# One product for the row sums of eight rows, a longer lag caught up near the end, and five small operations for twelve aggregations of moments

## The chip, the cores and the metric

The kernel runs on one core of one Trainium2 chip, all in float32. The metric is the device time of one execution in microseconds (us).

## The reference, cut to what matters

Two layers on `x` of shape (1, 384, 384, 128). The first is a triangle product with gates and two layer norms. The second, which is where the change lies, treats each of the 384 rows (384 positions of 128 channels) like this:

```python
left = pair @ W_left + b_left            # and W_eq, b_eq added to it
right = pair @ W_right + b_right
gate = jax.nn.sigmoid(pair @ W_gate + b_gate)
right_sum = jnp.sum(right, axis=2, keepdims=True)   # over the 384 positions of the row
out = left * right_sum * gate
out = out @ W_out + b_out
return _layer_norm(out + pair, ln_scale, ln_bias)    # over the 128 channels
```

`right_sum` is one vector of 128 channels for a row. The kernel sums pair over the positions first, and multiplies the sums by W_right.

## The kernel before, in words

The kernel has three stages: projections of the first layer (to about 1260 us), the triangle product, channel by channel (to about 1980 us), and the row stage, which goes through the 384 rows u and makes the end of the first layer and all of the second. P is 128, N is 384, C is 128, NB is 3 blocks of 128 positions, and R = 4 rows form a group that is loaded, normalised and stored together. The engines run the instructions in the order in which the code gives them (the schedule is manual), so the order of the row stage is that of the tuple `stages`: at each u, each stage is called for row u minus its lag.

One pass of the loop, with its lines:

- `load` (L505): every fourth u, SyncE starts the loads of gr, zr and xr for the group eight rows ahead (L512, L513, L522).
- `gate_product`, lag 3 (L968): VectorE (DVE) makes h = (pleft + b_left) x sg (L971).
- `turn_row`, lag 2 (L955): TensorE (PE) turns the row's pair (ptr, L560). ScalarE (ACT) copies it to pairT with an accumulated sum over the positions, which goes to column i of the group's tile `total` (L561).
- `out_weights`, lag 7 (L962): ACT scales W_out by the row's `right` column into w_o (L965).
- `layer_1`, lag 8 (L982): PE multiplies h by w_o (pf, three products, six PE passes, L987), and DVE adds pair (res, L988).
- `layer_0`, lag 0, and with it the statistics of the row eight back (L530): PE's py for row u (L537). On DVE three scalar_tensor_tensors on py (L543) alternate with three bn_stats of res (L548), then pair is made (L550), then three bn_aggr turn the statistics into mean and variance in `mv` (L553).
- `norm_factors`, lag 12 (L990): for a group of 4 rows x 3 blocks, GpSimd (POOL) makes rs = (variance + eps)^-0.5 (L995, L996) and off = -mean x rs (L998, L999).
- `normalise`, lag 13 (L1003): ACT makes res x rs + off, three a row (L1005).
- `project`, lag 2 (L1010): PE's pleft and pg from pairT (L1013, L1015), and ACT's sigmoid sg of pg (L1020). Where u is the first row of a group, the group before has all its sums: `right` adds a product of W_right with its 4 columns of `total` into the spare columns of pg's bank (L1026), and ACT copies it to the tile `right` with its bias (L1022).
- `store`, lag 17 (L1028): POOL multiplies the group by ln_scale (L1037) and adds ln_bias (L1038), and SyncE sends it out (L1042).

In the first rows, `project` and `gate_product` have one row more of lag; at row 6 `project` runs twice, and from there on the lag is as above. `behind` holds what is left of the stage before (on POOL, ACT and PE: L600 to L630, L595) and is advanced in each of the first rows, and then once in four.

[...] bn_stats leaves six numbers for a block of 128 channels: count, mean and the sum of squared deviations of its even elements, and the same of its odd ones; bn_aggr joins the two halves.

After the loop comes a tail written out by hand for the last rows. The last eight rows' statistics are made there with `statistics` (L1090, L1092) and their factors on DVE and ACT with `last_factors` (L1101 to L1110).

Of the kernel before, what the change touches and what calls it, by code (L numbers as in the profile page):

```python
# [9 lines left out]
FP = mybir.dt.float32  # L10
AF = mybir.ActivationFunctionType
ALU = mybir.AluOpType
# [8 lines left out]
def kernel(ctx: ExitStack, tc: tile.TileContext, ins, out: bass.AP):  # L21
# [89 lines left out]
    with tc.tile_pool(name="wprep", bufs=6) as wp, tc.tile_pool(name="p1s", bufs=3) as ps, tc.tile_pool(  # L111
# [49 lines left out]
        def norm_factors(n, c0=0, c1=CX, beside=nc.gpsimd):  # L161
            if n >= NT:
                return
            if n >= OLD:
                return turned_factors(n, c0, c1)
            mv, rstd, off = (tiles[n][k][:, c0:c1] for k in ("mv", "rstd", "off"))
            beside.tensor_scalar(rstd, mv[:, :, 1], EPS, None, ALU.add)
            beside.tensor_scalar(off, mv[:, :, 0], -1.0, None, ALU.mult)
            nc.gpsimd.tensor_tensor(rstd, rstd, mhalf[:, 0 : c1 - c0], ALU.pow)
            nc.gpsimd.tensor_tensor(off, off, rstd, ALU.mult)  # L170
            if c0 == 0:
                tiles[n]["zT"] = pz.tile([P, CX, C], FP, tag="zT", name=f"zn_{n}")
# [326 lines left out]
    nc.gpsimd.memset(s2, 0.0)  # L499
    LAST, AHEAD, BY_THIRDS, R, HELD = 8, 6, 6, 4, 16  # L500
    group = {}

    def load(u):
        if u % R:
            return  # L505
        load_pair(u)
        load_x(u)

    def load_pair(u):
        zr = pl.tile([P, R, NB, C], FP, tag="zr", name=f"zr_{u}")  # L510
        gr = pl.tile([P, R, NB, C], FP, tag="gr", name=f"gr_{u}")
        nc.sync.dma_start(out=gr, in_=G[u : u + R].rearrange("i (p q) c -> p i q c", q=NB))  # L512
        nc.sync.dma_start(out=zr, in_=Z[u : u + R].rearrange("i (p q) c -> p i q c", q=NB))  # L513
        g = {"z": zr, "g": gr}
        g["total"] = pl.tile([P, R], FP, tag="total", name=f"total_{u}", bufs=4)
        g["right"] = pl.tile([P, R], FP, tag="right", name=f"right_{u}", bufs=4)
        group[u // R] = g

    def load_x(u):
# [5 lines left out]
    def of(u):  # L525
        return group[u // R], u % R

    pairs = {}

    def layer_0(u, v, bank):  # L530

        now, past = 0 <= u < N, 0 <= v < N
        if now:
            g, i = of(u)
            py = bank(u)
            for q in range(NB):
                nc.tensor.matmul(  # L537
                    py[:, q, :], lhsT=g["x"][:, i, q * P : (q + 1) * P], rhs=w_o0, start=True, stop=True
                )
            pairs[u] = pairs_of.tile([P, NB, C], FP, tag="pair", name=f"pair_{u}")  # L540
        for q in range(NB):
            if now:
                nc.vector.scalar_tensor_tensor(  # L543
                    py[:, q, :], py[:, q, :], rs0[:, q, u : u + 1], g["g"][:, i, q, :], ALU.mult, ALU.mult
                )
            if past:
                b, k = of(v)
                nc.vector.bn_stats(b["st"][:, k, q, :], b["res"][:, k, q, :])  # L548
        if now:
            nc.vector.tensor_tensor(pairs[u], py, g["z"][:, i], ALU.add)  # L550
        if past:
            for q in range(NB):
                nc.vector.bn_aggr(b["mv"][:, k, q, :], b["st"][:, k, q, :])  # L553

    hs = {}

    def turn(u, ptr, pairT):
# [81 lines left out]
    with tc.tile_pool(name="p2", bufs=1, side="right", reuse_waits="tile") as p2, tc.tile_pool(  # L639
# [44 lines left out]
        def bank2(name):  # L684
            return pp2.tile([P, N], FP, tag="pm", name=name)
# [235 lines left out]
        held.close()  # L921
        work_of = ctx.enter_context(tc.tile_pool(name="work", bufs=1, reuse_waits="tile"))
        pl = ctx.enter_context(tc.tile_pool(name="p3l", bufs=3, reuse_waits="tile"))
        pairs_of = ctx.enter_context(tc.tile_pool(name="p3r", bufs=12, reuse_waits="tile"))
        behind, rest = None, [NB - 2]
        for ib in range(NB):
            for d in range(C - LAST, C):
                if ib == NB - 1 and d == C - LAST:
                    load_x(0)
                    load_x(R)  # L930
                product(d, ib)
                if behind:
                    advance(behind)
                if ib == NB - 2 and d in (C - LAST, C - LAST + 1):
                    load_pair((d + LAST - C) * R)
                if ib == NB - 1 and d in (C - 4, C - 3):
                    layer_0(d + 4 - C, -1, lambda u: bank2(f"py_{u}").rearrange("p (q c) -> p q c", q=NB))
                if ib == NB - 1 and d == C - 2:
                    turn(0, bank2("ptr3_0"), pairs_of.tile([P, N], FP, tag="pair", name="pairT_0"))
            add_squares()  # L940
            behind = (deviation(ib), deviation(ib, rest), None)[ib]
# [4 lines left out]
    with tc.tile_pool(name="p3s", bufs=4, reuse_waits="tile") as ps, tc.tile_pool(  # L946
# [4 lines left out]
        name="p3q", bufs=2, space=PSUM, reuse_waits="tile"  # L951
    ) as plp, tc.tile_pool(name="p3f", bufs=2, space=PSUM, reuse_waits="tile") as pfp:
        wos = {}

        def turn_row(u):  # L955
            if u:
# [10 lines left out]

        def gate_product(u):  # L968
            pleft, sg = hs[u]
            h = ps.tile([P, N], FP, tag="h", name=f"h_{u}", bufs=8)  # L970
            nc.vector.scalar_tensor_tensor(h, pleft, b_left, sg, ALU.add, ALU.mult)  # L971
            hs[u] = h

        def results(u):
            g, i = of(u)
            if i == 0:
                g["res"] = pg3.tile([P, R, NB, C], FP, tag="res", name=f"res_{u}")
                g["st"] = pg3.tile([P, R, NB, 6], FP, tag="st3", name=f"st3_{u}")
                g["mv"] = pg3.tile([P, R, NB, 2], FP, tag="mv3", name=f"mv3_{u}")
            return g, i  # L980

        def layer_1(u):  # L982
# [5 lines left out]
            nc.vector.tensor_tensor(g["res"][:, i], pf, pairs.pop(u), ALU.add)  # L988

        def norm_factors(u):  # L990
            if u % R:
                return
            g, _ = of(u)
            rs = pg3.tile([P, R, NB], FP, tag="rs1", name=f"rs1_{u}")
            nc.gpsimd.tensor_scalar(rs, g["mv"][:, :, :, 1], EPS, None, ALU.add)  # L995
            nc.gpsimd.tensor_tensor(rs, rs, mhalf[:, 0 : R * NB].rearrange("p (r q) -> p r q", r=R), ALU.pow)  # L996
            off = pg3.tile([P, R, NB], FP, tag="off", name=f"off_{u}")
            nc.gpsimd.tensor_tensor(off, g["mv"][:, :, :, 0], rs, ALU.mult)  # L998
            nc.gpsimd.tensor_scalar(off, off, -1.0, None, ALU.mult)  # L999
            g["rs"], g["off"] = rs, off  # L1000

        def normalise(u):
            g, i = of(u)  # L1003
# [6 lines left out]
        def project(u):  # L1010
            pairT = hs[u]
            pleft = plp.tile([P, N], FP, tag="pleft", name=f"pleft_{u}")
            nc.tensor.matmul(pleft, lhsT=w_left, rhs=pairT, start=True, stop=True)  # L1013
            pg = pgp.tile([P, 512], FP, tag="pg", name=f"pg_{u}")
            nc.tensor.matmul(pg[:, 0:N], lhsT=w_gate, rhs=pairT, start=True, stop=True)  # L1015
            g = group.get(u // R - 1) if u % R == 0 else None
            if g:
                right(g, pg)
            sg = ps.tile([P, N], FP, tag="sg3", name=f"sg3_{u}")
            nc.scalar.activation(sg, pg[:, 0:N], AF.Sigmoid, bias=b_gate)  # L1020
            if g:
                nc.scalar.activation(g["right"], pg[:, N : N + R], AF.Identity, bias=b_right)  # L1022
            hs[u] = pleft, sg

        def right(g, pg):
            nc.tensor.matmul(pg[:, N : N + R], lhsT=w_right, rhs=g["total"], start=True, stop=True)  # L1026

        def store(u, n=R):  # L1028

# [11 lines left out]
        def send(u, n, res):  # L1041
            nc.sync.dma_start(out=y_out[u : u + n].rearrange("i (p q) c -> p i q c", q=NB), in_=res)  # L1042

        stages = (
            (load, -2 * R), (gate_product, 3), (turn_row, 2), (out_weights, 7), (layer_1, 8), (layer_0, 0),
            (norm_factors, 12), (normalise, 13), (project, 2), (store, 17),
        )
        load(2 * R)
        behind = chain(
            rest_of_deviation(*rest, lambda: pfp.tile([P, N], FP, tag="pf", name="pr_1")),  # L1050
            last_deviation(NB - 1, lambda: pfp.tile([P, N], FP, tag="pf", name="pr_2")),
        )
        for u in range(2, N):
            for stage, lag in stages:

                if stage in (gate_product, project):
                    if u < lag + R:
                        lag += 1
                    elif u == lag + R:
                        stage(u - lag - 1)  # L1060
                if stage is layer_0:
                    stage(u, u - 8, lambda u: pyp.tile([P, NB, C], FP, tag="py", name=f"py_{u}"))
                elif 0 <= u - lag < N:
                    stage(u - lag)
                if stage is layer_1 and (u < 12 or u % R == 1):
                    advance(behind)

# [6 lines left out]
        def bank(u):  # L1074
            pool, tag = ((pyp, "py"), (pfp, "pf"), (plp, "pleft"))[(D - 1 - u) // 2]
            banks[u] = pool.tile([P, NB, C], FP, tag=tag, name=f"end_{u}")
            return banks[u]
# [66 lines left out]
            nc.vector.tensor_tensor(res, banks[u], over(ln_b, NB), ALU.add)  # L1144
            nc.sync.dma_start(out=y_out[u].rearrange("(p q) c -> p q c", q=NB), in_=res)

        norm_factors(D - 12)
        turn_row(D - 2)
        gate_product(D - 3)
        out_weights(D - 7)  # L1150
        layer_1(D - 8)
        statistics(D - 8)
        turn_row(D - 1)
        out_weights(D - 6)
# [89 lines left out]
```

## Time and profile before

| | |
|---|---|
| runs of the kernel | median 3152.47 us of 3 (3152.08 to 3152.94) |
| the profiled execution | 3152.62 us, its span 3150.8 us |
| granted TensorE clock | 0.998 |
| busy, of the span: PE, DVE, ACT, POOL | 99%, 93%, 70%, 81% |
| the row stage, 2200 to 2400 us: busy of 200 us, PE, DVE, ACT, POOL | 200.00, 200.00, 175.58, 192.13 |
| the same stretch: weight loads on PE; DMA's share | 162.19; 0.78 |
| DRAM traffic in the row stage | 256 to 267 GB/s |

The time of an execution is its span (first to last instruction) and about 1.8 us around it. In a row of the profile, `L543 DVE SCALAR_TENSOR_TENSOR py<-py,acc,gr` is an instruction of line 543 on DVE that writes tile py from py, acc and gr; then come a count, the busy time, the mean duration in ns, and the idle time ahead of it with what ended that. PE multiplies float32 in two passes, each with its weight load (PEld), so a product has two PE instructions, and three products have six. In a timeline the first number is the start, the second the duration, both in us. Instructions overlap a little: on DVE the next one starts some 0.08 us before the end of the one ahead, so that the cost of an instruction is the time from its start to the next one's start. The chain of waits is the work that set the end, followed back from the last instruction.

### The profile page before, as it was taken

What the parts mean: (1) busy time and instruction counts of PE and PEld (TensorE: products, weight loads), DVE (VectorE), ACT (ScalarE), POOL (GpSimd) and SP (SyncE); (2) the same over time, 40 slices, a digit from 0 to 9 for tenths busy, and PEclk for the clock granted to TensorE, in tenths of its full rate; (3) what the DMA queues carried; (4) which work ended last, traced back from release to release, by engine and by line L of the source; (5) the groups of instructions that cost most, each with busy time, mean ns of one, the idle gap of its engine ahead of it and who ended that gap; (6) DMA issues with size and microseconds to landing.
All of it is one profiled execution on the core that took longest, in us unless ns stands there. A gap on an engine that the chain in (4) does not pass through costs nothing.

```text
span 3150.8 us, 57517 instructions
## 1 busy us (share of the span) xinstructions
PE 3130.0 (99%) x15723; PEld 2229.0 (71%) x15723; DVE 2928.8 (93%) x9353; ACT 2219.7 (70%) x5816; POOL 2564.9 (81%) x2753
## 2 busy tenths in 40 slices
PE   9999999999999999999999999999999999999998
PEld 6555555555555555788888887788888888888886
DVE  7999999999999998788888888999999999999999
ACT  7666666666666666555555554688888888888888
POOL 7888888888888886777777775599999998888887
PEclk9999999999999999999999999999999999999999
DMA  7999999999999999999999999677777777777774
GB/s 250 370 363 371 371 363 372 360 351 365 368 371 363 371 359 346 352 328 327 326 331 329 326 322 308 229 264 264 259 269 259 270 260 268 265 258 271 257 271 153
DMA packets 427742, 983.15 MB, mean 312 GB/s; under 512 B 40848, under 2 KB 335376, under 8 KB 382240
## 3 DMA queue, kind: packets, MB, share of 16 engines
q1 hardware_dynamic: 385344, 752.64, 68.8%
q0 software_dynamic: 41504, 226.58, 18.1%
q8 instruction: 130, 2.13, 0.3%
q14 instruction: 188, 1.54, 0.1%
q10 hardware_dynamic: 576, 0.26, 0.0%
HBM read 526.39 MB, written 452.98 MB: 311 GB/s over the span
## 4 chain that ended last, share of the span: by engine, by line
PE 98%; ACT 1%; DMA 1%; DVE 0%; POOL 0%; issue 0%; SPq 0%; DVEq 0%; POOLq 0%
PE py L537 8%; PE pgo L271 8%; PE pf L987 8%; PE pleft L1013 8%; PE pg L1015 8%; PE pga L309 8%; PE pb L309 8%; PE pgb L309 8%; PE pa L309 8%; PE pm L840 7%; PE ptr L560 4%; PE be L840 4%; PE al L840 4%; PE ga L840 4%; PE pm L702 1%; PE p L840 1%
## 5 line engine op out<-in xcount | busy, mean ns | idle before, releaser
L1005 ACT ACTIVATE res<-res,off,rs 128x128 f32<-128x128 f32 x1134 | 474.8, 485 | 1.0
L317 ACT ACTIVATE sga<-pga,c_L_conv_bga 128x512 f32<-128x512 f32 x288 | 197.9, 687 | 326.2 <-PE pga L309 326.1
L543 DVE SCALAR_TENSOR_TENSOR py<-py,acc,gr 128x128 f32<-128x128 f32 x1152 | 391.1, 340 | 0.6
L271 PEld LDWEIGHTS pgo<-wC_go,xT 128*128 128x128 f32 x2208 | 287.5, 192 | 124.8 <-issue 65.3
L1038 POOL TENSOR_TENSOR res<-res,r_L_conv_ln_bias 128x1536 f32<-128x1536 f32 (+1 forms) x96 | 326.8, 3404 | 7.5
L1020 ACT ACTIVATE sg<-pg,c_L_conv_b_gate 128x384 f32<-128x384 f32 x384 | 223.3, 581 | 150.7 <-PE pg L1015 100.7
L1037 POOL TENSOR_TENSOR res<-res,r_L_conv_ln_scale 128x1536 f32<-128x1536 f32 (+1 forms) x96 | 327.0, 3406 | 0.5 <-ACT res L1005 0.5
L235 POOL TENSOR_TENSOR acc<-xt,r_L_conv_b_out 128x2048 f32<-128x2048 f32 x72 | 326.0, 4527 | 0.2
L537 PE MATMUL py<-w_o,xr 128*128 128x128 f32 x2304 | 320.0, 275 | 0.0
L987 PE MATMUL pf<-w_o,h 128*128 128x128 f32 x2280 | 316.7, 275 | 0.0
L548 DVE BATCH_NORM_STATS2 st<-res 128x6 f32<-128x128 f32 x1128 | 313.3, 278 | 0.0
L1013 PE MATMUL pleft<-pairT,m_L_conv_W_left 128*128 128x384 f32 x768 | 311.5, 487 | 0.3 <-ACT pairT L561 0.3
L1015 PE MATMUL pg<-pairT,m_L_conv_W_gate 128*128 128x384 f32 x768 | 310.6, 486 | 0.0
L355 DVE SCALAR_TENSOR_TENSOR bt<-pb,c_L_conv_bb,sgb 128x512 f32<-128x512 f32 x288 | 216.1, 750 | 83.5 <-ACT sgb L317 38.6
L537 PEld LDWEIGHTS py<-w_o,xr 128*128 128x128 f32 x2304 | 288.3, 192 | 0.8
L271 PE MATMUL pgo<-wC_go,xT 128*128 128x128 f32 x2208 | 288.5, 275 | 0.0
L840 PE MATMUL pm<-ab 128*128 128x384 f32 x708 | 286.3, 486 | 1.5 <-ACT pm L783 1.5
L987 PEld LDWEIGHTS pf<-w_o,h 128*128 128x128 f32 x2280 | 284.6, 192 | 0.5
L309 PE MATMUL pga<-xT,wC_ga 128*128 128x512 f32 x552 | 282.6, 594 | 0.0
L309 PE MATMUL pb<-xT,wC_b 128*128 128x512 f32 x552 | 281.9, 592 | 0.0
L309 PE MATMUL pgb<-xT,wC_gb 128*128 128x512 f32 x552 | 281.9, 592 | 0.0
L309 PE MATMUL pa<-xT,wC_a 128*128 128x512 f32 x552 | 281.9, 592 | 0.0
(245 smaller groups left out, 8221.5 us busy)
## 6 DMA issues: line engine op xcount, KB each, us to landing
A<-at POOLq DMA_DIRECT2D x144, 512.0 KB, 10.4
Z<-acc POOLq DMA_DIRECT2D x72, 1024.0 KB, 10.8
gr<-G SPq DMA_DIRECT2D x96, 768.0 KB, 6.2
zr<-Z SPq DMA_DIRECT2D x96, 768.0 KB, 7.8
xr<-X SPq DMA_DIRECT2D x96, 768.0 KB, 8.4
X<-xd SPq DMA_DIRECT2D x381, 192.0 KB, 6.7
xt<-in_x_dram SPq DMA_DIRECT2D x71, 1024.0 KB, 7.9
out_dram<-res SPq DMA_DIRECT2D x93, 768.0 KB, 4.2
```

Of the source, the lines that this page charges most:

```text
L235: nc.gpsimd.tensor_tensor(zb, tiles[n]["x"], over(b_out, CX), ALU.add)
L271: nc.tensor.matmul(pgo[:, c, :], lhsT=zT[:, c, :], rhs=wT["go"], start=True, stop=True)
L309: nc.tensor.matmul(pk, lhsT=wT[k], rhs=zT, start=True, stop=True)
L537: nc.tensor.matmul(py[:, q, :], lhsT=g["x"][:, i, q * P : (q + 1) * P], rhs=w_o0, start=True, stop=True)
L543: nc.vector.scalar_tensor_tensor(py[:, q, :], py[:, q, :], rs0[:, q, u : u + 1], g["g"][:, i, q, :], ALU.mult, ALU.mult)
L840: nc.tensor.matmul(columns(to), lhsT=x, rhs=y, start=start, stop=True, skip_group_check=True)
L987: nc.tensor.matmul(pf[:, q, :], lhsT=h[:, q * P : (q + 1) * P], rhs=w_o, start=True, stop=True)
L1005: nc.scalar.activation(g["res"][:, i, q, :], g["res"][:, i, q, :], AF.Identity, bias=g["off"][:, i, q : q + 1], scale=g["rs"][:, i, q : q ...
L1013: nc.tensor.matmul(pleft, lhsT=w_left, rhs=pairT, start=True, stop=True)
L1015: nc.tensor.matmul(pg[:, 0:N], lhsT=w_gate, rhs=pairT, start=True, stop=True)
L1037: nc.gpsimd.tensor_tensor(flat, flat, over(ln_s, n * NB), ALU.mult)
L1038: nc.gpsimd.tensor_tensor(flat, flat, over(ln_b, n * NB), ALU.add)
```

## The change

Three things change in the row stage.

1. **The right product** is made once for eight rows up to row 328, and once for four after that. Two groups share one tile of 8 sums and one of 8 right columns.
2. **The lag** of `out_weights`, `layer_1` and all that follows is four rows longer (a row's layer_1 comes 12 rows after its layer_0 instead of 8), since a row's right column may come four rows later. The four rows are caught up: at u = 341, 348, 355 and 362, `layer_1` is called for two rows, with two `out_weights` one row ahead and two `normalise` six rows behind. The tables `due` and `plan` say which rows are due at which u. `normalise` stands one row further behind `layer_1` than before, and so does `store`; at u = 383, `normalise` is called twice. `h` has 12 buffers instead of 8, `pair` 14 instead of 12.
3. **The moments.** Instead of three bn_aggr for each row, a generator `moments` joins the halves for a whole group (12 columns) in five DVE operations and one Square on ACT, spread over the row that ends the group and the next one: after each of the calls of `gate_product`, `out_weights` and `layer_1`, it is advanced by a step. Two of its intermediate results lie in the spare columns of py's bank, which is now taken whole. `norm_factors` on POOL is an add, the pow and a multiplication (three operations instead of four). The last eight rows still use bn_aggr.

```diff
+    BY_FOUR, CAUGHT_UP = 328, (330, 338, 346, 354)
+    def octet(u):
+        return 2 * R if u < BY_FOUR else R
+    def products_at(v):
+        return v + 12 - sum(v >= k for k in CAUGHT_UP)
...
-        g["total"] = pl.tile([P, R], FP, tag="total", name=f"total_{u}", bufs=4)
-        g["right"] = pl.tile([P, R], FP, tag="right", name=f"right_{u}", bufs=4)
+        n = octet(u)
+        if u % n == 0:
+            g["sums"], g["rights"] = (
+                pl.tile([P, 2 * R], FP, tag=k, name=f"{k}_{u}", bufs=4)[:, 0:n] for k in ("total", "right")
+            )
+        else:
+            g["sums"], g["rights"] = (group[u // R - 1][k] for k in ("sums", "rights"))
+        g["total"], g["right"] = (g[k][:, u % n : u % n + R] for k in ("sums", "rights"))
...
-            if past:
-                b, k = of(v)
+            for b, k in map(of, past):
                 nc.vector.bn_stats(b["st"][:, k, q, :], b["res"][:, k, q, :])
         if now:
             nc.vector.tensor_tensor(pairs[u], py, g["z"][:, i], ALU.add)
-        if past:
-            for q in range(NB):
-                nc.vector.bn_aggr(b["mv"][:, k, q, :], b["st"][:, k, q, :])
+        if past and past[-1] % R == R - 1:
+            ending[0] = moments(past[-1], whole[:, N:])
+            advance(ending[0])
...
+        def moments(u, spare):
+            n = R * NB
+            other_mean, other_part = (spare[:, k * n : k * n + n].rearrange("p (r q) -> p r q", r=R) for k in (0, 1))
+            g, _ = of(u)
+            mean, part, other_m, other_p = (g["st"][:, :, :, k] for k in (1, 2, 4, 5))
+            var, off, apart = (pg3.tile([P, R, NB], FP, tag=k, name=f"{k}_{u}") for k in ("rs1", "off", "apart"))
+            g["rs"], g["off"], g["apart"] = var, off, apart
+            nc.vector.tensor_scalar(other_mean, other_m, -0.5, None, ALU.mult)
+            yield
+            nc.vector.scalar_tensor_tensor(apart, other_mean, 2.0, mean, ALU.mult, ALU.add)
+            nc.vector.scalar_tensor_tensor(off, mean, -0.5, other_mean, ALU.mult, ALU.add)
+            nc.vector.tensor_scalar(other_part, other_p, 1.0 / C, EPS, ALU.mult, ALU.add)
+            yield
+            nc.scalar.activation(apart, apart, AF.Square, scale=0.5)
+            yield
+            nc.vector.scalar_tensor_tensor(var, part, 1.0 / C, other_part, ALU.mult, ALU.add)
+            yield
...
         def norm_factors(u):
-            if u % R:
-                return
             g, _ = of(u)
-            rs = pg3.tile([P, R, NB], FP, tag="rs1", name=f"rs1_{u}")
-            nc.gpsimd.tensor_scalar(rs, g["mv"][:, :, :, 1], EPS, None, ALU.add)
+            rs, off = g["rs"], g["off"]
+            nc.gpsimd.tensor_tensor(rs, rs, g["apart"], ALU.add)
             nc.gpsimd.tensor_tensor(rs, rs, mhalf[:, 0 : R * NB].rearrange("p (r q) -> p r q", r=R), ALU.pow)
-            off = pg3.tile([P, R, NB], FP, tag="off", name=f"off_{u}")
-            nc.gpsimd.tensor_tensor(off, g["mv"][:, :, :, 0], rs, ALU.mult)
-            nc.gpsimd.tensor_scalar(off, off, -1.0, None, ALU.mult)
-            g["rs"], g["off"] = rs, off
+            nc.gpsimd.tensor_tensor(off, off, rs, ALU.mult)
...
-            g = group.get(u // R - 1) if u % R == 0 else None
+            g = group[u // R - 1] if u and u % octet(u - 1) == 0 else None
             if g:
                 right(g, pg)
...
         def right(g, pg):
-            nc.tensor.matmul(pg[:, N : N + R], lhsT=w_right, rhs=g["total"], start=True, stop=True)
+            n = g["sums"].shape[1]
+            nc.tensor.matmul(pg[:, N : N + n], lhsT=w_right, rhs=g["sums"], start=True, stop=True)
...
-            (load, -2 * R), (gate_product, 3), (turn_row, 2), (out_weights, 7), (layer_1, 8), (layer_0, 0),
-            (norm_factors, 12), (normalise, 13), (project, 2), (store, 17),
+            (load, -2 * R), (gate_product, 3), (turn_row, 2), (out_weights, None), (layer_1, None), (layer_0, 0),
+            (norm_factors, None), (normalise, None), (project, 2), (store, None),
         )
+        for v in range(N):
+            u = products_at(v)
+            plan(out_weights, u - 1, v)
+            plan(layer_1, u, v)
+            plan(normalise, u + 6 if u + 6 < N else N - 1 if u + 5 < N else u + 5, v)
+            if v % R == 0:
+                plan(norm_factors, products_at(v + R - 1) + 1, v)
+                plan(store, u + 10, v)
...
+                if stage in (gate_product, out_weights, layer_1):
+                    advance(ending[0])
...
-        norm_factors(D - 12)
         turn_row(D - 2)
         gate_product(D - 3)
+        advance(ending[0])
         out_weights(D - 7)
+        advance(ending[0])
         layer_1(D - 8)
+        advance(ending[0])
+        norm_factors(D - 12)
         statistics(D - 8)
```

More of the change, by code (lines that the diff above doesn't have):

```diff
@@ L528, with layer_0 @@
     pairs = {}
-    def layer_0(u, v, bank):
-        now, past = 0 <= u < N, 0 <= v < N
+    def layer_0(u, past, bank):
+        now = u < N
         if now:
             g, i = of(u)
-            py = bank(u)
+            whole = bank(u)
+            py = whole[:, 0:N].rearrange("p (q c) -> p q c", q=NB)
             for q in range(NB):
@@ L550, in layer_0 @@
             nc.vector.tensor_tensor(pairs[u], py, g["z"][:, i], ALU.add)
-        if past:
-            for q in range(NB):
-                nc.vector.bn_aggr(b["mv"][:, k, q, :], b["st"][:, k, q, :])
+        if past and past[-1] % R == R - 1:
+            ending[0] = moments(past[-1], whole[:, N:])
+            advance(ending[0])
+    ending = [iter(())]
     hs = {}
@@ L923 @@
         pl = ctx.enter_context(tc.tile_pool(name="p3l", bufs=3, reuse_waits="tile"))
-        pairs_of = ctx.enter_context(tc.tile_pool(name="p3r", bufs=12, reuse_waits="tile"))
+        pairs_of = ctx.enter_context(tc.tile_pool(name="p3r", bufs=14, reuse_waits="tile"))
         behind, rest = None, [NB - 2]
@@ L936 @@
                 if ib == NB - 1 and d in (C - 4, C - 3):
-                    layer_0(d + 4 - C, -1, lambda u: bank2(f"py_{u}").rearrange("p (q c) -> p q c", q=NB))
+                    layer_0(d + 4 - C, (), lambda u: bank2(f"py_{u}"))
                 if ib == NB - 1 and d == C - 2:
@@ L969, in gate_product @@
             pleft, sg = hs[u]
-            h = ps.tile([P, N], FP, tag="h", name=f"h_{u}", bufs=8)
+            h = ps.tile([P, N], FP, tag="h", name=f"h_{u}", bufs=12)
             nc.vector.scalar_tensor_tensor(h, pleft, b_left, sg, ALU.add, ALU.mult)
@@ L977, in results @@
                 g["res"] = pg3.tile([P, R, NB, C], FP, tag="res", name=f"res_{u}")
-                g["st"] = pg3.tile([P, R, NB, 6], FP, tag="st3", name=f"st3_{u}")
-                g["mv"] = pg3.tile([P, R, NB, 2], FP, tag="mv3", name=f"mv3_{u}")
+                g["st"] = pg3.tile([P, R, NB, 6], FP, tag="st3", name=f"st3_{u}", bufs=2)
+                if u >= N - 2 * R:
+                    g["mv"] = pg3.tile([P, R, NB, 2], FP, tag="mv3", name=f"mv3_{u}", bufs=2)
             return g, i
@@ L1021, in project @@
             if g:
-                nc.scalar.activation(g["right"], pg[:, N : N + R], AF.Identity, bias=b_right)
+                n = octet(u - 1)
+                nc.scalar.activation(g["rights"], pg[:, N : N + n], AF.Identity, bias=b_right)
             hs[u] = pleft, sg
         def right(g, pg):
-            nc.tensor.matmul(pg[:, N : N + R], lhsT=w_right, rhs=g["total"], start=True, stop=True)
+            n = g["sums"].shape[1]
+            nc.tensor.matmul(pg[:, N : N + n], lhsT=w_right, rhs=g["sums"], start=True, stop=True)
         def store(u, n=R):
@@ L1044, with plan @@
         stages = (
-            (load, -2 * R), (gate_product, 3), (turn_row, 2), (out_weights, 7), (layer_1, 8), (layer_0, 0),
-            (norm_factors, 12), (normalise, 13), (project, 2), (store, 17),
-        )
+            (load, -2 * R), (gate_product, 3), (turn_row, 2), (out_weights, None), (layer_1, None), (layer_0, 0),
+            (norm_factors, None), (normalise, None), (project, 2), (store, None),
+        )
+        due = {}
+        def plan(stage, u, v):
+            due.setdefault((stage, u), []).append(v)
+        for v in range(N):
[6 more added lines that the diff above has]
+                plan(store, u + 10, v)
         load(2 * R)
@@ L1053 @@
         for u in range(2, N):
+            past = due.get((layer_1, u), ())
             for stage, lag in stages:
@@ L1060 @@
                         stage(u - lag - 1)
-                if stage is layer_0:
-                    stage(u, u - 8, lambda u: pyp.tile([P, NB, C], FP, tag="py", name=f"py_{u}"))
+                if lag is None:
+                    for v in due.pop((stage, u), ()):
+                        stage(v)
+                elif stage is layer_0:
+                    stage(u, past, lambda u: pyp.tile([P, 512], FP, tag="py", name=f"py_{u}"))
                 elif 0 <= u - lag < N:
                     stage(u - lag)
+                if stage in (gate_product, out_weights, layer_1):
+                    advance(ending[0])
                 if stage is layer_1 and (u < 12 or u % R == 1):
```

## The prediction

> **What bounds the kernel now.** First the page's busy line and its chain of waits, for the engine that sets the end.
>
> ```profile
> PE 3130.0 (99%) x15723; PEld 2229.0 (71%) x15723; DVE 2928.8 (93%) x9353; ACT 2219.7 (70%) x5816; POOL 2564.9 (81%) x2753
> ...
> PE 98%; ACT 1%; DMA 1%; DVE 0%; POOL 0%; issue 0%; SPq 0%; DVEq 0%; POOLq 0%
> ```
>
> PE is the chain for 98% of the span. The change touches only the row stage (from about 1980 us), so next the chain of waits cut to its end, which lists PE's pieces one after the other (start, length):
>
> ```profile
> 3056.05 0.65 PE pleft L1013 x2
> 3056.69 0.65 PE pg L1015 x2
> 3057.34 0.33 PE ptr L560 x3
> 3057.66 0.67 PE pf L987 x6
> 3058.34 0.67 PE py L537 x6
> 3059.01 0.65 PE pleft L1013 x2
> 3059.65 0.65 PE pg L1015 x2
> 3060.30 0.12 PE pg L1026 x2
> ...
> 3062.14 0.65 PE pleft L1013 x2
> ```
>
> From one pleft to the next a row takes 2.96 us without a gap; the row that holds the right product takes 3.13. Four rows: 3 x 2.960 + 3.133 = 12.013, or 3.003 a row. One right product costs 0.173 us (in the trace's nanoseconds, 3133 less 2960), not the 0.12 of its own piece. Then DVE's timeline near the end, because DVE is the nearest second:
>
> ```profile
> 3118.26 0.30 DVE L553 BATCH_NORM_AGGREGATE mv<-st 128x2 f32<-128x6 f32 x3
> 3118.48 0.58 DVE L971 SCALAR_TENSOR_TENSOR h<-pleft,c_L_conv_b_left,sg 128x384 f32<-128x384 f32 x1
> ...
> 3121.48 0.58 DVE L971 SCALAR_TENSOR_TENSOR h<-pleft,c_L_conv_b_left,sg 128x384 f32<-128x384 f32 x1
> ...
> 3134.17 0.17 DVE L1106 SCALAR_TENSOR_TENSOR t<-r,few 128x12 f32<-128x12 f32 x1
> 3134.37 0.17 DVE L1107 TENSOR_TENSOR few<-t,few 128x12 f32<-128x12 f32 x1
> 3134.58 0.18 DVE L1108 SCALAR_TENSOR_TENSOR few<-few,r 128x12 f32<-128x12 f32 x1
> 3134.79 0.17 DVE L1109 COPY rs<-few 128x12 f32<-128x12 f32 x1
> 3134.88 0.16 DVE L1110 SCALAR_TENSOR_TENSOR off<-mv,few 128x12 f32<-128x12 f32 x1
> 3134.95 0.69 DVE L1090 BATCH_NORM_STATS2 st<-end 128x6 f32<-128x128 f32 x3
> ```
>
> From h to h DVE takes 3.00 us with no idle time (3.005 over the stage, from the nanoseconds). So DVE is full too, level with PE: taking work from PE alone would gain nothing. The three aggregations of a row cost 0.22 (3118.26 to 3118.48). The lower rows price an operation on 12 columns: 0.07 to 0.09 from start to start where it needn't wait for the one before (L1109, L1110), 0.20 to 0.21 where it must (L1106 to L1108).
>
> **Part 1, right products on PE.** Before, the loop makes one at each of rows 4, 8, ... 380: 95. After: at 8, 16, ... 328 (41), then at 332 ... 380 (13): 54. Its 8 columns instead of 4 I take as free: the 128x4 product's time is weight loads (2 x 190 ns busy) and a fixed part. 41 x 0.173 = **-7.1 us**, if nothing else becomes the bound.
>
> **Part 2, moments on DVE.** Removed for four rows: 4 x 0.22 = 0.88. Added: five operations. In the built program the first (after pair) and the fourth (after off) wait for the DVE instruction just before them; the other three have work between. Bounds: 5 x 0.073 = 0.37 to 5 x 0.21 = 1.05. I take 3 x 0.08 + 2 x 0.20 = 0.64, by those rows. DVE then needs 12.02 - 0.88 + 0.64 = 11.78 for four rows, 2.945 a row, against PE's 2.960 + 0.173/8 = 2.982. So PE stays the bound with 0.037 a row to spare, and part 1's gain is real. DVE becomes the bound when the five cost more than 0.88 - (12.02 - 11.93) = 0.79, which is 0.158 each.
>
> [...]
>
> The Square that ACT gets per group is the price of the 128x12 sd (start to start 0.06 to 0.09); ACT waits 134.9 us for pg's products in 373 rows from 2010 to 3120 us, 0.36 a row, and that hides it. The sigmoid's table has Square in it: L579 loads it at 1971.95 and the L722 squares follow at 1973.37 without a load. POOL loses L999 (0.26 and a gap of 0.08) and swaps L995 (0.25) for an add near L998's 0.21. Its four-row round up to about row 200 was 12.0 (pow 2.30, scale and shift 6.92, L628 1.67, rest) and becomes 11.6, within PE's 11.93. The factors are ready some 2 us before ACT's first normalise, which now stands a row later. SP's store moves one row back ahead of the next loads, which have eight rows of lead; the res buffers' 16 rows of lead shrink to 14 where rows are caught up, against a life of some 40 us. All these cost nothing; if that cover fails, a wait of about 1 us per group there shows on ACT.
>
> **Part 3, four rows of lag at the start.** Rows 8 to 11 lose their pf (0.67 each), paid later in four rows (341, 348, 355, 362) with two: +2.7. What comes back at the start is less, because without pf nothing covers ACT's pairT:
>
> ```profile
> 1990.66 0.28 PE L1026 MATMUL pg<-total,m_L_conv_W_right 128*128 128x4 f32 x2
> ...
> 1992.33 0.91 PE L1013 MATMUL pleft<-pairT,m_L_conv_W_left 128*128 128x384 f32 x2 [0.34 <-ACT pairT L561]
> ```
>
> This is row 7 of before, the one without a pf at the final lag: PE waits. The loop is sg to pairT 0.48, pairT to pleft 0.73 (1991.60 to 1992.33), pleft to the next sg 1.59 (to 1993.92): 2.80 against 2.96. So rows 8 to 10 save 0.16 each, row 11 (after a right product) nothing, and row 7 saves 0.37 for row 4's right product, of which 0.17 is counted. Net 2.7 - 0.5 - 0.2 = **+2.0** (bounds 0, if those rows ran at the 2.29 of rows 3 and 4, and 2.7).
>
> **Part 4, ACT in the catch-up.** Rows 347, 354, 361 and 368 get two rows of normalise: three more L1005, 1.16 from start to start (3127.09 to 3128.24 in the tail), and the first three a second w_o, 0.29 (3118.48 to 3118.77). Less ACT's idle 0.38 of a plain row (ahead of the sg at 2501.44), plus the Square's 0.09, sg comes 1.2 late. pairT has 0.26 to spare before pleft (end 2502.49, 0.16 from end to pleft as at 1992.33, pleft at 2502.91), and the second pf of 348, 355 and 362 adds 0.67: about 0.2 to 0.3 of PE wait each, more where Square waits for a DVE that the double row made late. Row 369 has no second pf: 0.9 - 0.3 = 0.6. Sum **+1.5**, bounds 0.5 and 4.5 (each lateness in full).
>
> **Part 5, the last row.** Row 383 also gets two normalises. Its sg is on the path (3123.54, idle 0.28 before it), and pairT, ptr, pleft and ACT to the end follow it: 1.16 - 0.28 = **+0.9**. The later factors of the last full group (pow 2.3) are ready before ACT's normalise at 3132.35.
>
> Sum: -7.1 + 2.0 + 1.5 + 0.9 = -2.7 on the profiled execution's 3152.62 (span 3150.8 and 1.8 around it): 3149.9. It stands 0.15 above the median of 3152.47, so the forecast is **3149.8**.
>
> **Rivals.**
> A, the edges are nearly free: early rows at 2.29 as rows 3 and 4 show, no stall in the catch-up; -7.1 + 0.9: 3146.3, down to 3145.4 without part 5. Against it: rows 3 and 4 still have the longer lag to pleft, and row 7 waits.
> B, slower: all five DVE operations pay the dependent 0.21. DVE then needs 12.02 - 0.88 + 1.05 = 12.19, 3.047 a row, 0.044 over today's pace for some 370 rows: +16, near 3168. [...] Against it: three have another operation between. It decides from 0.158 each on.
> C, ACT's lateness hits PE in full: +4.5 instead of 1.5: 3152.8, no change.
>
> **Chances.** Forecast 0.64, A 0.18, C 0.10, B 0.08. About 0.2% (6.3 us) is what a measurement of this kernel can tell from no change: faster needs under 3146.2, nearly half of A with a little of the forecast's tail, 0.10; slower is B, 0.08; the rest 0.82. The range leaves out B and the low end of A: 3145.8 to 3152.9.
>
> **What would show it.** Right: pleft to pleft 2.96 in seven rows of eight and 3.13 in the eighth; DVE with idle time ahead of h or py; the operations of the first and fourth moments at 0.2 and the others near 0.08; pleft waiting for pairT in rows 8 to 11; sg late in the four catch-up rows. Wrong: a PE wait on DVE in the steady rows, an h-to-h of 3.0 or more without idle time (B), or POOL's factors ending ACT's idle time ahead of normalise.

## The result, and the profile after

The changed kernel takes 3160.62 us (median of 10 runs, 3160.26 to 3161.26), the kernel before, run beside it, 3152.68 (10 runs). The ratio is 1.0026, with a 95% interval of 1.0016 to 1.0035: 8 us slower, where 2.7 us faster was forecast, and above the top of the range (3152.9). The profiled execution's span is 3158.6 us.

The page's busy line and chain of waits:

```profile
PE 3129.4 (99%) x15641; PEld 2222.3 (70%) x15641; DVE 2917.0 (92%) x8695; ACT 2232.6 (71%) x5869; POOL 2533.6 (80%) x2659
...
PE 95%; ACT 1%; POOL 1%; DVE 1%; DMA 1%; issue 0%; ACTq 0%; SPq 0%; DVEq 0%; POOLq 0%
```

PE's busy time is 0.6 us lower in a span 7.8 us longer, and POOL and DVE, with nothing in the chain before, now hold 1% each: 39 and 36 us in which they are on the path, 4 and 6 before. The steady rows are not where it happened. PE's timeline near 2500 us (start, duration):

```profile
2498.90 0.81 PE L1042 MATMUL pleft<-pairT,m_L_conv_W_left 128*128 128x384 f32 x2
...
2501.86 0.81 PE L1042 MATMUL pleft<-pairT,m_L_conv_W_left 128*128 128x384 f32 x2
...
2503.15 0.28 PE L1057 MATMUL pg<-total,m_L_conv_W_right 128*128 128x8 f32 x2
...
2504.99 0.81 PE L1042 MATMUL pleft<-pairT,m_L_conv_W_left 128*128 128x384 f32 x2
...
2507.95 0.81 PE L1042 MATMUL pleft<-pairT,m_L_conv_W_left 128*128 128x384 f32 x2
```

A row takes 2.96 us, one with a right product 3.13, and those now come every eighth row: as forecast, the 128x8 product costs what the 128x4 one did. To find where the time went, line up the two traces by rows: when does pleft of row r start, less when it did before? The row stage itself starts up to 1 us earlier or later from one profile to the next, so the difference at row 0 is taken off. The table counts rows by their pleft. Where the text below says "row 348" of a stretch on PE or of a call, it means the pass u = 348 of the loop, whose pleft is that of row 346. In us:

| row | 12 | 328 | 347 | 354 | 361 | 370 | 382 | end of span |
|---|---|---|---|---|---|---|---|---|
| changed kernel | -0.8 | -7.1 | -5.3 | -2.0 | +4.5 | +6.7 | +7.4 | +7.7 |
| e1, store first | -0.8 | -7.1 | -5.4 | -3.8 | -2.3 | -0.8 | -0.1 | +0.1 |
| e2, five res buffers | -0.9 | -7.4 | -5.7 | -4.1 | -1.8 | +1.4 | +2.2 | +2.4 |
| e3, moments alone | 0.0 | 0.0 | 0.0 | 0.0 | 0.0 | 0.0 | +0.7 | +0.9 |
| e4, e1 with bn_aggr | -0.8 | -2.7 | -0.6 | +0.6 | +1.9 | +2.7 | +3.7 | +3.7 |
| e5, e1 and Square later | -0.8 | -7.1 | -5.5 | -4.6 | -3.7 | -3.1 | -2.3 | -2.3 |
| e6, e1 and longer lag at the start | -2.8 | -9.8 | -8.0 | -6.4 | -4.9 | -3.5 | -2.7 | -2.5 |
| e7, e1 and normalise spread | -0.8 | -7.1 | -5.8 | -4.7 | -3.6 | -3.0 | -3.0 | -2.7 |
| e8, all four edits | -2.9 | -9.8 | -8.4 | -7.8 | -7.1 | -6.8 | -6.5 | -6.0 |

Up to row 328 the changed kernel is 7.1 us ahead. Between there and row 370, the catch-up, it loses 13.7, of which 2.7 are the four pf that were put off. Eleven us are waits. The waits of the stage from 2010 to 3120 us name most of them (engine, line, what it waited for: us in all, times, longest):

```profile
DVE res L1022 <- DMA out_dram<-res: 6.8, 2, 3.5
...
PE pf L1021 <- DVE rs L985: 4.2, 2, 2.4
...
DVE res L1022 <- PE pf L1021: 2.2, 1, 2.2
...
ACT res L1034 <- POOL off L1029: 1.7, 1, 1.7
```

DVE waits for a store: the buffer that a new group's res is to go into has not been sent out. PE then waits for DVE. None of this was in the kernel before. The wait of 2.2 us that the view puts down to PE's pf is a store's too: that row's pf had ended at 3081.00, and res starts at 3084.01, 0.12 us after the store of the buffer's last group landed, as it does in the other two (3.2 and 3.5 us). So DVE stands 9.0 us for stores, in three places. At one of these places, in the timeline of DVE and PE:

```profile
3033.93 0.56 DVE L1022 TENSOR_TENSOR res<-pf,pair 128x384 f32<-128x384 f32 x1 [3.22 <-DMA out_dram<-res]
...
3034.41 0.16 DVE L985 SCALAR_TENSOR_TENSOR rs<-st,py 128x12 f32<-128x12 f32 x1
...
3034.64 0.91 PE L1021 MATMUL pf<-w_o,h 128*128 128x128 f32 x6 [1.88 <-DVE rs L985]
```

And why was the buffer late? It is that of group 328, whose last normalise ended at 3012.93. POOL's timeline:

```profile
3006.32 3.45 POOL L1069 TENSOR_TENSOR res<-res,r_L_conv_ln_bias 128x1536 f32<-128x1536 f32 x1
3009.74 0.21 POOL L1027 TENSOR_TENSOR rs<-rs,apart 128x12 f32<-128x12 f32 x1
3010.03 2.28 POOL L1028 TENSOR_TENSOR rs<-rs,mhalf 128x12 f32<-128x12 f32 x1
3012.39 0.21 POOL L1029 TENSOR_TENSOR off<-off,rs 128x12 f32<-128x12 f32 x1
3019.51 0.21 POOL L1027 TENSOR_TENSOR rs<-rs,apart 128x12 f32<-128x12 f32 x1 [6.91 <-DVE rs L985]
3019.80 2.27 POOL L1028 TENSOR_TENSOR rs<-rs,mhalf 128x12 f32<-128x12 f32 x1
3022.14 0.21 POOL L1029 TENSOR_TENSOR off<-off,rs 128x12 f32<-128x12 f32 x1
3022.32 3.45 POOL L1068 TENSOR_TENSOR res<-res,r_L_conv_ln_scale 128x1536 f32<-128x1536 f32 x1
```

Two sets of factors follow each other, 332's and 336's. Ahead of the second POOL stands idle for 6.91 us until DVE has group 336's last row, and behind it, in POOL's order, waits group 328's scale, whose data has lain ready since 3012.93. It starts 9.4 us late. In the steady rows factors come at u = 0 and scales at u = 2 (modulo 4). In the catch-up the due rows move: `plan(norm_factors, products_at(v + R - 1) + 1, v)` puts 336's factors at u = 350, `plan(store, u + 10, v)` puts 328's store at u = 350 too, and the tuple of stages has norm_factors first. The same meets groups 336 and 344, whose scales start 12.3 and 12.5 us after their data. It doesn't meet 352: its store comes at u = 371, the factors of 360 at u = 372, and its scale is 3.5 us late only because POOL is still behind.

### The profile page after: what moved, and what is told of

Same layout as the page of the kernel before. It is cut to its first block, busy times and chain, and to the rows that moved or that the text cites. A ratio compares the mean times of both kernels' runs of the same rounds, so it can differ in the third digit from the quotient of the medians.

```text
span 3158.6 us, 56583 instructions
## 1 busy us (share of the span) xinstructions
PE 3129.4 (99%) x15641; PEld 2222.3 (70%) x15641; DVE 2917.0 (92%) x8695; ACT 2232.6 (71%) x5869; POOL 2533.6 (80%) x2659
## 4 chain that ended last, share of the span: by engine, by line
PE 95%; ACT 1%; POOL 1%; DVE 1%; DMA 1%; issue 0%; ACTq 0%; SPq 0%; DVEq 0%; POOLq 0%
PE pgo L271 8%; PE pga L309 8%; PE pa L309 8%; PE pb L309 8%; PE pgb L309 8%; PE py L552 7%; PE pleft L1042 7%; PE pf L1021 7%; PE pg L1044 7%; PE pm L855 7%; PE ptr L575 4%; PE be L855 4%; PE al L855 4%; PE ga L855 4%; PE pm L717 1%; PE p L855 1%
## 5 line engine op out<-in xcount | busy, mean ns | idle before, releaser
L558 DVE SCALAR_TENSOR_TENSOR py<-py,acc,gr 128x128 f32<-128x128 f32 x1152 | 404.9, 351 | 0.9
L562 DVE BATCH_NORM_STATS2 st<-res 128x6 f32<-128x128 f32 x1128 | 326.4, 290 | 0.0
```

The costliest lines, as they stand in the source:

```text
L558: nc.vector.scalar_tensor_tensor(py[:, q, :], py[:, q, :], rs0[:, q, u : u + 1], g["g"][:, i, q, :], ALU.mult, ALU.mult)
```

## The experiments

Three theories of the loss. P: POOL's order in the catch-up. Q: ACT's doubled work holds PE, and POOL only follows (rival C of the prediction, larger). R: four res buffers are too few in any order. Two more runs (e3, e4) test what the prediction got right, that DVE and PE had to be relieved together, and four (e5 to e8) what is left of the loss. Run beside e1 to e4, the kernel before takes 3152.06 us, beside e5 to e8 3152.09, and beside the changed kernel it took 3152.68; so a run is set against the changed kernel by its distance from the kernel before. The intervals are some 0.09% to each side, 2.8 us: gains of 2.4 to 2.8 us are no more than that, and what shows them is the place in the table where they arise.

**e1, store first.** In the changed kernel:

```diff
-            (norm_factors, None), (normalise, None), (project, 2), (store, None),
+            (store, None), (norm_factors, None), (normalise, None), (project, 2),
```

> The changed kernel with one edit: in the tuple of stages, store stands ahead of norm_factors, so that on POOL the scale of a finished group goes ahead of the factors of a later one. Theory P (POOL's order): in the changed kernel the scale of groups 328, 336, 344 and 352 starts some 9 to 14 us after its data is ready, because the factors of the group two further on stand ahead of it and wait for their last row; the four res buffers then come free late, and DVE waits for the store. Without that, the catch-up (rows 336 to 370) loses the 2.7 us of the moved pf and some 1.5 us of ACT lateness instead of 13.7: 3150 to 3152.5 us. Theory Q (ACT): the doubled w_o and normalise hold PE by themselves and POOL only follows: 3159 to 3161. Theory R (four res buffers are too few for 14 rows in any order): DVE still waits for the store, 3156 to 3160.

Measured 3152.26 us (11 runs; before 3152.06, ratio 1.0001, 0.9992 to 1.0010): 0.2 us slower than the kernel before instead of 7.9. One tuple's order is worth 7.7 us, or 7.5 by the table. POOL in the same place:

```profile
3011.38 0.21 POOL L1029 TENSOR_TENSOR off<-off,rs 128x12 f32<-128x12 f32 x1
3011.98 3.47 POOL L1068 TENSOR_TENSOR res<-res,r_L_conv_ln_scale 128x1536 f32<-128x1536 f32 x1 [0.39 <-ACT res L1034]
...
3018.93 0.23 POOL L1027 TENSOR_TENSOR rs<-rs,apart 128x12 f32<-128x12 f32 x1
```

The scale starts as soon as ACT is done, and 336's factors, placed behind it, start 0.7 us after DVE starts the last operation on their data (3018.19). DVE waits for no store any more. P stands; Q and R fall as the main cause. What is left of the catch-up's loss (6.3 from row 328 to 370, of which 2.7 for pf) is 3.6 us: the subject of e5 and e7.

**e2, five res buffers.** In the changed kernel, POOL's order as it was:

```diff
-                g["res"] = pg3.tile([P, R, NB, C], FP, tag="res", name=f"res_{u}")
+                g["res"] = pg3.tile([P, R, NB, C], FP, tag="res", name=f"res_{u}", bufs=5)
```

> The changed kernel with five res buffers instead of four, POOL's order as it is. Theory P and theory R: DVE no longer waits for the store of the group four back, so most of the 11 us of stalls goes: 3150.5 to 3153.5 us; the late scales on POOL remain and cost nothing but the length of the queue; what differs from the run with store first is the hold of the factors behind late scales (ACT waited 1.7 us for off). Theory Q: 3159 to 3161.

Measured 3154.51 (ratio 1.0008, 0.9999 to 1.0017): 2.5 us slower than the kernel before, 5.5 better than the changed kernel, 1.0 outside the expectation and 2.3 short of e1. DVE's waits for the store are gone, and the remaining way shows in the waits from 3000 to 3125 us:

```profile
ACT res L1034 <- POOL off L1029: 5.5, 3, 2.0
...
PE pleft L1042 <- ACT pairT L576: 3.8, 5, 1.1
```

POOL's late scales also hold the next factors; ACT waits for those, and its pairT comes late for PE. So the one inversion had two ways to PE, through the buffers and through the factors, and a fifth buffer closes only one.

**e3, the moments alone.** The changed kernel with `BY_FOUR = 0` and `return v + 8` in `products_at`: a right product for every four rows, no longer lag, no catch-up.

> The change of the moments alone: a right product for four rows and the lag of 8 as before, no catch-up; moments, normalise and store one row later as in the changed kernel. Theory (PE is the bound at 3.003 us a row, DVE was level with it): DVE gets idle time, PE's pace stays, 0 to 1 us from the kernel before, 0.9 more for the double normalise of the last row: 3152.0 to 3154.0 us. Rival (PE was held by DVE, 3.005 a row, or by its PSUM buffers): faster by 1 to 7 us. Rival (the moments themselves cost PE through py's bank or ACT's Square): slower by more than 2 us.

Measured 3152.88 (ratio 1.0003, 0.9994 to 1.0011). By rows it runs level with the kernel before to the last row (PE 3.003 us a row in both), and loses 0.7 to 0.9 in the tail, at row 383's double normalise. DVE's relief by itself gives nothing, since PE takes its 3.003 anyway. DVE now follows PE at a fixed distance: h starts 2.25 us after its row's pleft from row 60 to row 324, where before that distance crept up from 2.39 to 2.60 in the first 180 rows.

**e4, bn_aggr in place of the moments.** e1 with the old lines: in `layer_0`

```diff
-        if past and past[-1] % R == R - 1:
-            ending[0] = moments(past[-1], whole[:, N:])
-            advance(ending[0])
+        for b, k in map(of, past):
+            for q in range(NB):
+                nc.vector.bn_aggr(b["mv"][:, k, q, :], b["st"][:, k, q, :])
```

and `norm_factors` as before, with `mv` for every group.

> The run with store first, but with the twelve bn_aggr of before in place of the moments: right product for eight rows, lag 12 and catch-up remain. Theory (DVE is level with PE in the kernel before, so taking work from PE alone gains nothing): DVE sets the pace at 3.005 us a row, and the 7 us of right products don't show; 3152 to 3156 us. Rival (PE alone is the bound, DVE's missing idle time is only its queue): as fast as the run with store first, within 0.7 us.

Measured 3155.73 (ratio 1.0012, 1.0004 to 1.0021), 3.5 us behind e1. It shows how a lead is lost: from row 20 to row 100 PE does run at 2.982 us a row, and DVE's h falls behind pleft from 2.52 to 4.30 us. PE turns a row's pair two rows after DVE makes it. At row 20 the transposes (ptr) start 1.9 us after the pair's end, at row 60 0.9, and from row 100 on 0.15 to 0.16. In the timelines of DVE and PE at one of the later rows:

```profile
2932.68 0.60 DVE L564 TENSOR_TENSOR pair<-py,zr 128x384 f32<-128x384 f32 x1
...
2933.43 0.52 PE L575 MATMUL ptr<-ident,pair 128*128 128x128 f32 x3
```

So the distance between pair and ptr is used up. From row 220 to row 324 PE's pace is 3.002, near DVE's 3.005. The difference at row 328 is 2.7 us instead of 7.1; from there to row 370 it loses 5.5, e1 6.3. With e3 this shows that the two halves of the change need each other.

**e5, Square later.** e1, with ACT's Square moved behind the row's normalise:

```diff
-            nc.scalar.activation(apart, apart, AF.Square, scale=0.5)
-            yield
             nc.vector.scalar_tensor_tensor(var, part, 1.0 / C, other_part, ALU.mult, ALU.add)
             yield
+            nc.scalar.activation(apart, apart, AF.Square, scale=0.5)
+            yield
...
-                if stage in (gate_product, out_weights, layer_1):
+                if stage in (gate_product, layer_1, normalise):
```

(and one more yield after the first operation, and norm_factors behind normalise). It aims at this. ACT's timeline in e1, three rows after a double row:

```profile
3016.10 0.40 ACT L998 ACTIVATE w_o<-m_L_conv_W_out,right 128x128 f32<-128x128 f32 x1
3017.53 0.21 ACT L983 ACTIVATE apart<-apart 128x12 f32<-128x12 f32 x1 [1.03 <-DVE apart L979]
...
3018.80 0.56 ACT L1049 ACTIVATE sg<-pg,c_L_conv_b_gate 128x384 f32<-128x384 f32 x1
```

And PE's timeline in e1 for the same row:

```profile
3016.53 0.81 PE L1042 MATMUL pleft<-pairT,m_L_conv_W_left 128*128 128x384 f32 x2
3020.12 0.91 PE L1042 MATMUL pleft<-pairT,m_L_conv_W_left 128*128 128x384 f32 x2 [0.29 <-ACT pairT L576]
```

Three rows after a double row DVE is still late; ACT stands 1.03 us at Square, sg and pairT are late, and PE's row, which holds a right product, takes 3.59 instead of 3.13.

> The run with store first, and ACT's Square moved behind the row's normalise (the fourth DVE step then goes before it, and norm_factors behind normalise), so that ACT no longer stands at Square for a DVE that a double row made late. Theory S (Square in ACT's order is what stalls rows 351, 358 and 365, 0.3 to 0.6 us each, with some more in the double rows themselves): 1.2 to 2 us faster than the run with store first, 3150.3 to 3151.1. Rival (ACT has no time for its work in these rows in any order): within 0.5 us of it. Rival (the later factors make normalise wait): slower.

Measured 3149.86 (ratio 0.9993, 0.9984 to 1.0001), 2.4 us under e1, a little more than expected. Rows 351, 358 and 365, which took 3.59, 3.29 and 3.26 us in e1, take 3.13, 2.96 and 2.96.

**e6, longer lag at the start.** e1, and in the loop

```diff
-                    if u < lag + R:
+                    if u < lag + 2 * R:
                         lag += 1
-                    elif u == lag + R:
+                    elif u == lag + 2 * R:
```

> The run with store first, with the longer lag of project and gate_product kept for four rows more at the start (up to row 10 instead of 6). Theory (rows without a pf at the final lag are held by the loop sg, pairT, pleft at 2.80 us; with one row more of lag PE runs them at 2.29): rows 7 to 9 come back to 2.29, 1.5 us faster than the run with store first, 3150.5 to 3151. Rival (the first rows are held by something else, DVE or the loads): within 0.5 us of it.

Measured 3149.49 (ratio 0.9992, 0.9983 to 1.0001), 2.8 us under e1, where 1.5 was expected. PE's timeline in the changed kernel's first rows:

```profile
1994.91 0.91 PE L1042 MATMUL pleft<-pairT,m_L_conv_W_left 128*128 128x384 f32 x2 [0.24 <-ACT pairT L576]
...
1997.70 0.91 PE L1042 MATMUL pleft<-pairT,m_L_conv_W_left 128*128 128x384 f32 x2 [0.24 <-ACT pairT L576]
```

And PE's timeline in the same stretch of e6:

```profile
1989.37 0.81 PE L1042 MATMUL pleft<-pairT,m_L_conv_W_left 128*128 128x384 f32 x2
...
1991.66 0.81 PE L1042 MATMUL pleft<-pairT,m_L_conv_W_left 128*128 128x384 f32 x2
```

2.79 us a row with a wait against 2.29 without. The table's rows 5 to 8 gain, four of them and not three, so 2.0 by row 12. Another 0.6 is three small waits of 0.2 to 0.3 (near rows 24, 112 and 185) that the changed kernel and e1 have and e6 doesn't; their cause was not followed.

**e7, normalise spread.** e1, with at most four of normalise's activations in a row, in their order, and row 370's last two in ACT's idle times of the tail:

```diff
+        thirds, came = {}, []
+        for u in range(N):
+            came += [(v, q) for v in range(N) if products_at(v) + 6 == u for q in range(NB)]
+            if u == N - 1:
+                came.append((N - 14, 0))
+            thirds[u], came = came[:4], came[4:]
...
+        normalise_part(D - 14, (1,))
         turn_row(D - 1)
         out_weights(D - 6)
+        normalise_part(D - 14, (2,))
         project(D - 2)
```

> The run with store first, with the doubled normalise spread: at most four of its 128x128 activations in a row, so that a double takes three rows, and in the last rows two of the extra three go to ACT's idle times in the tail. Theory (three more L1005 in one row make sg late by more than pairT's 0.26 and the second pf can take; one more is hidden in ACT's 0.38): the stalls of rows 348, 355, 362 and 369 (2.4 us with their followers) and the 0.75 of row 383 go: 2 to 3 us faster than the run with store first, 3149.3 to 3150.3. Rival (the late rows come from the double w_o and from DVE): within 0.7 us of it.

Measured 3149.66 (ratio 0.9992, 0.9983 to 1.0001), 2.6 us under e1. The rows 348, 355, 362 and 369 with the double work took 3.9, 4.1, 3.9 and 3.9 us in e1, from pleft to pleft, and take 3.63, 3.80, 3.63 and 3.14 here. The first three are what such a row takes without a wait (3.63 with two pf, 3.80 with a right product besides). Row 369 has neither, and 0.2 of its wait is left. The loss at the table's row 382 is gone.

**e8, all four edits.** The edits of e1, e5, e6 and e7 in one kernel.

> All four edits together: store first, Square behind normalise, the longer lag at the start kept to row 10, the doubled normalise spread. If the three theories hold and their stalls are separate: 1.4 + 1.5 + 2.7 below the run with store first, 3146 to 3147.5 us, some 5 us (0.17%) below the kernel before. If they share one stall, 3148 to 3150.

Measured 3146.30 us (11 runs, 3145.79 to 3146.80; before 3152.09, ratio 0.9981, 0.9972 to 0.9989): 5.8 us faster than the kernel before, and 13.7 better than the changed kernel. The gains over e1 are 2.4, 2.8 and 2.6 alone, 7.8 together, and 6.0 were reached. The table places the overlap: up to row 328 e8 has all of e6's gain (2.7). From there to the end of the span e5 gains 2.4 us on e1 and e7 2.8, and e8 only 3.4. So e5 and e7 relieve in part the same rows.

## Why the prediction was wrong, point by point

**The failed step** is the last paragraph of part 2: "SP's store moves one row back ahead of the next loads ... the res buffers' 16 rows of lead shrink to 14 where rows are caught up, against a life of some 40 us. All these cost nothing". The life of 40 us was that of the steady rows. In the catch-up POOL has another order: the due times of the factors move with rows v + 3, those of the stores with v, and a wait for group 336's last row came to stand ahead of group 328's store. Group 328's res was first written at 2986.04, and the next write to that buffer could only start at 3033.93, when the store had landed: a life of 47.9 us. It was wanted 3.22 us earlier, 44.7 us after the first write, since the caught-up rows shorten the 16 rows of lead. The waits are 3.2, 3.5 and 2.2 us, for the stores of groups 328, 336 and 344. e1 shows what the late stores cost with all that hung on them: 7.7 us, where the prediction had put nothing. Its bound if that cover fails, "a wait of about 1 us per group" on ACT, was short and on another engine, and no rival ended there. e1's expectation names group 352 as well; the trace shows three. The prediction looked for a wait that takes the place of the one removed on PE, DVE and ACT, and counted POOL's work, but did not list POOL's instructions in the order that they have in rows 340 to 370.

**Part 1, right products: right.** Forty of the 41 fall between rows 12 and 328, 6.9 us; measured there 6.2 (-0.8 to -7.1 in the table), nearly all of the rest in the three small waits (0.6).

**Part 2, moments: the conclusion right, by a hair.** PE did stay the bound. The h-to-h distances in a group are 2.80, 2.80, 3.03 and 3.28, together 11.91 us, the same in e8's catch-up, where DVE is up to 1.5 us later than in the steady rows and runs without a stop. So 11.91, and not 11.78, is what DVE needs for four rows, against PE's 11.93: a margin of 0.02 where the sum had 0.15. The five operations add 0.23 + 0.48 = 0.71 to two plain rows, against 0.64. And a plain row takes 2.80, not the 2.785 of the sum (3.005 less 0.22): without the aggregations ahead of it, h takes 0.52 us to the next start instead of 0.50. Two of DVE's lines before:

```profile
2499.45 0.59 DVE L971 SCALAR_TENSOR_TENSOR h<-pleft,c_L_conv_b_left,sg 128x384 f32<-128x384 f32 x1
2499.95 0.55 DVE L988 TENSOR_TENSOR res<-pf,pair 128x384 f32<-128x384 f32 x1
```

In e4, with the aggregations back, it is 0.50 again; why it changes is not shown. The sum had no term for that. DVE's timeline in the changed kernel:

```profile
2506.77 0.56 DVE L564 TENSOR_TENSOR pair<-py,zr 128x384 f32<-128x384 f32 x1
2507.37 0.18 DVE L977 TENSOR_SCALAR py<-st 128x12 f32<-128x12 f32 x1
2507.46 0.61 DVE L1004 SCALAR_TENSOR_TENSOR h<-pleft,c_L_conv_b_left,sg 128x384 f32<-128x384 f32 x1
2507.98 0.16 DVE L979 SCALAR_TENSOR_TENSOR apart<-py,st 128x12 f32<-128x12 f32 x1
2508.06 0.17 DVE L980 SCALAR_TENSOR_TENSOR off<-st,py 128x12 f32<-128x12 f32 x1
2508.26 0.18 DVE L981 TENSOR_SCALAR py<-st 128x12 f32<-128x12 f32 x1
2508.37 0.56 DVE L1022 TENSOR_TENSOR res<-pf,pair 128x384 f32<-128x384 f32 x1
2508.85 0.17 DVE L985 SCALAR_TENSOR_TENSOR rs<-st,py 128x12 f32<-128x12 f32 x1
```

L979 to L980 is 0.08, L980 to L981, which waits for it, 0.20. And pair to L977 is 0.60 where pair to h is 0.46. So in this trace an operation that must wait for the one before it starts 0.12 to 0.14 us later than one that needn't.

**Part 3, the start: right.** Row 12 was to be 0.9 us ahead (0.5 + 0.2 + 0.17), and is 0.8; the rows took 2.79 to 2.80, as the loop said. e6 shows that the bound named for it (2.29 a row) can be had.

**Part 4, ACT in the catch-up: the mechanism right, the size not.** 3.6 us in e1 instead of 1.5, inside its bounds. The double rows and the ones right behind them cost 2.2. The term missed is Square waiting for a late DVE three rows later: 1.1 in rows 351, 358 and 365, and 0.3 in the rows behind them; it was named only for the double rows. (ACT's waits of 134.9 us fall on 369 rows and not 373: 0.37 a row.)

**Part 5, the last row: right.** 0.9 forecast; 0.7 to 0.8 in the changed kernel, e1 and e3 by the table's row 382, 0.9 to 1.0 by the end of the span. In e7 it is none by row 382 and 0.3 by the end.

**Rivals.** A's bound of free edges (3146.3) is what e8 reaches by removing most of those costs. B, the five operations at 0.21, did not come about, and the kernel was slower all the same: another mechanism at another place. C is rejected as the main cause by e1.

## What to carry to other kernels

Where the order on an in-order engine is written by due times, list that engine's instructions for the irregular stretch, not only the steady one, and look at each instruction that waits: what ready work stands behind it? Two engines that are level must be relieved together, and the lead that one gains alone lasts only until the distance between what one makes and the other needs is used up (here 1.9 us, in about 80 rows). Work that is put off should be paid back in pieces that fit into each engine's idle time per row (one activation more, 0.39 us in 0.38, and not three).

## What the runs showed of the hardware

The length of DVE's records was no measure of its load in these runs. In the changed kernel the same instructions last longer than before (py 351 ns on average instead of 340, bn_stats 290 instead of 278), but the next one starts as soon: 0.25 to 0.26 us after py and 0.20 after bn_stats, in both. In e4, where DVE sets PE's pace, the records are the longest (374 and 313 ns), at the same spacing. What an instruction costs is to be read from start to start.

DVE's slack in e3 doesn't show as idle time either. There DVE needs 11.91 us for four rows and PE takes 12.01. The 0.10 between them stands in one place of a group, where py starts 0.56 us after res instead of 0.46. Since DVE's records overlap by some 0.08 us, next to nothing of that is idle time in the view.
